# Two attention layers of a gated block: the last tiles' softmax divided after the product with the values

## The chip, the cores and the metric

The kernel runs on one core of one Trainium2 chip. The metric is the device time of one execution in microseconds. Times inside the execution are from its profile, counted from the start of the span.

## The reference

Eight sublayers work one after the other on a residual stream `x` of 4 x 256 tokens by 256 features. Each normalises the stream, computes something, and adds it back times `tanh` of a gate. The change is in the third and fourth attention (called layers 2 and 3 below); what follows them is a quantised linear layer (layer 2) and a mixture of 8 experts with a shared expert (layer 3).

```python
def _L2_xattn_ref(q, latent_kv, Wq, Wkv_expand, Wout):      # layer 3 is the same
    qp = q @ Wq.T
    k, v = jnp.split(latent_kv @ Wkv_expand.T, 2, axis=-1)
    # 16 heads of 16 features
    scores = jnp.einsum('bhqd,bhkd->bhqk', qh, kh) * inv_sqrt_d
    scores = jnp.where(causal, scores, jnp.finfo(scores.dtype).min)
    attn = jax.nn.softmax(scores, axis=-1)
    out = jnp.einsum('bhqk,bhkd->bhqd', attn, vh)
    return out.transpose(0, 2, 1, 3).reshape(b, sq, H) @ Wout.T
...
x = x + jnp.tanh(g_xattn[2]) * _L2_xattn_ref(_layernorm(x), ctx_512, ...)
x = x + jnp.tanh(g_ffn[2]) * _L2_ffn_ref(_layernorm(x), ...)       # rounds rows to int8 steps
x = x + jnp.tanh(g_xattn[3]) * _L3_xattn_ref(_layernorm(x), ctx_512, ...)
x = x + jnp.tanh(g_ffn[3]) * _L3_ffn_ref(_layernorm(x), ...)       # router, 8 experts, shared expert
```

There are 64 keys per batch, so one query tile has 16 heads x 64 keys = 1024 scores in each of its 128 rows.

## The kernel before

The 1024 tokens are 8 tiles of 128 rows, `x[0]` to `x[7]`, in two groups of four (group 0 and group 1). The residual stream stays on chip. Matrix products are in float32 unless a row says bf16.

`attention23` does layers 2 and 3. For each tile there are these steps, named as in the code:

- `scores(t)`: products of queries and keys into a PSUM tile `wide` (line 1115; on even tiles the causal mask is added by a product, line 1105), then on DVE the row maximum of each head (line 1130) and the subtraction into `attn` (line 1132, two halves), then on ACT the exponential (line 1141).
- `weights(e)`: on DVE the sum of each head (line 496) and its reciprocal (line 497), then the division of the 128x1024 tile on POOL (line 501). For the last tile half of it is done on DVE (`shared=True`).
- `transposed_pairs` (`turn`): eight 128x128 transposes on PE (line 516), copied by ACT to `attnT` (line 517), two heads in each.
- `context(t, aT)`: eight products of values with `attnT`, each 32 columns wide, into four strips of a PSUM tile `mm` (line 1148), copied by ACT to `ctxTok` (line 1157). The values are laid out block by block for two heads, so the outcome is already transposed for the next product.
- `output(cT)`: products with the output weights (line 1165); `gated_add` adds it to `x[t]` on DVE (line 527).

`in_flight_parts` writes these steps out over the tiles, with tile `t` in its turn two rounds after its scores. In the version before, tiles 0 to 4 have turn, context and output in one round; from tile 5 on, the output of a tile follows the next tile's turn. `beside` is work of other steps, one piece per round: the queries of group 1, in layer 2 also the keys and values of layer 3 (lines 1040 and 1056), and at the end of layer 2 the layer norm of group 0 (round 8) and its rounding for the quantised layer (round 9, `rounded(0)`, lines 2048 to 2055).

The framework turns this into one queue of instructions per engine, ahead of the run. What is emitted sooner has the higher priority, and among instructions that its own estimate holds ready the one of highest priority comes next; `behind(a, b)` only forces an order. On the chip each queue runs in order. Score tiles and `attnT` share six buffers (`t4`), `mm` has four PSUM buffers and `wide` has two.

`kept_busy` issues products of the identity with a weight (line 522) whose outcome is not used; there are 7 and 2 of them in the quantised layer and 1 in layer 3 at tile 2.

After layer 2 comes `ffn2`: group 0's rounded tiles are transposed and multiplied (lines 2071 and 2080), added to `x` on POOL (line 2085); then group 1 is normalised (pow on POOL, line 439; ACT, line 452), rounded and multiplied; group 0's norm for layer 3 follows (square root on ACT, line 441, reciprocal on DVE, line 444), its transposes (line 467) and queries. After layer 3 come the norms of both groups, the router (line 1199) and, beside it, the shared expert (lines 482 and 1842), then the chosen experts.

Of the kernel before, what the change touches and what calls it, by code (L numbers as in the profile page):

```python
# [30 lines left out]
F32 = mybir.dt.float32  # L31
# [5 lines left out]
ALU = mybir.AluOpType  # L37
AX = mybir.AxisListType

P = 128  # L40
B, S, D = 4, 256, 256
T = B * S
NT = T // P
TH = 512
NG = T // TH
TPG = TH // P
L, DC = 64, 64
NH, DK, CQ, CQH, R = 16, 128, 192, 96, 64
NP = NH // 2
# [48 lines left out]
def tile_flamingo(ctx: ExitStack, tc: tile.TileContext, a: dict, out: bass.AP):  # L98
    nc = tc.nc

    const = ctx.enter_context(tc.tile_pool(name="const", bufs=1))
# [4 lines left out]
    def ps_mm():  # L106
        return psum.tile([P, 512], F32, tag="mm", name="mm", bufs=4)

    def ps_wide():
        return psum.tile([P, 2, 512], F32, tag="wide", name="wide", bufs=2)  # L110

    def t4(shape, name, dtype=F32):
        return sb.tile(shape, dtype, tag="t4", name=name, bufs=6)
# [27 lines left out]
    def behind(later, sooner):  # L141

        tc.add_manual_dep(
            later.ins,
            sooner.ins.name,
            mybir.DependencyInfo(mybir.DependencyClass.NoSync, mybir.DependencyReason.DATA),
            reason="not sooner",
        )

    def side_by_side(products):  # L150

        last = None
        for product in products:
            with tc.high_priority(AT_ONCE) if last else nullcontext():
                made = product()
            if last:
                behind(made, last)
            last = made
        return last
# [26 lines left out]
    nc.gpsimd.memset(ones, 1.0)  # L186
    eps = const.tile([P, 1], F32, tag="eps", name="eps")
    nc.gpsimd.memset(eps, EPS)
    power = const.tile([P, 1], F32, tag="power", name="power")
    nc.gpsimd.memset(power, -0.5)  # L190
    root = small([P, 1], "root", 1)
# [300 lines left out]
    def weights(e, shared=False):  # L492

        groups, n = e.shape[1], e.shape[2]
        sm = sb.tile([P, 16], F32, tag="sm", name="sm", bufs=3)[:, :groups]
        nc.vector.tensor_reduce(sm, e, AX.X, ALU.add)  # L496
        made = nc.vector.reciprocal(sm, sm)  # L497
        parts = [(nc.vector, slice(0, groups // 2)), (nc.gpsimd, slice(groups // 2, groups))]
        for engine, part in parts if shared else [(nc.gpsimd, slice(0, groups))]:
            one = e[:, part]  # L500
            engine.tensor_tensor(one, one, sm[:, part].unsqueeze(2).to_broadcast(list(one.shape)), ALU.mult)  # L501
        return made
# [5 lines left out]
    def transposed_pairs(e):  # L508

        aT = t4([P, NP, P], "attnT")  # L510
        ev = e.rearrange("p h l -> p (h l)")
        for half in range(2):
            ps = ps_mm()
            for i in range(4):
                pr = half * 4 + i
                nc.tensor.transpose(ps[:, i * P : (i + 1) * P], ev[:, pr * P : (pr + 1) * P], ident)  # L516
            nc.scalar.copy(aT[:, half * 4 : half * 4 + 4, :].rearrange("p i t -> p (i t)"), ps)  # L517
        return aT

    def kept_busy(n, ps, last):  # L520
        for _ in range(n):
            made = nc.tensor.matmul(ps, ident, loaded["L3"][:, :TH], start=True, stop=True)
            behind(made, last)
            last = made

    def gated_add(t, ps, gate):
        return nc.vector.scalar_tensor_tensor(x[t], ps, gate, x[t], ALU.mult, ALU.add)  # L527
# [15 lines left out]
    def in_flight_parts(scores, turn, context, output, gate, beside):  # L543

        made, ctx, outs = {}, {}, {}

        def add(t):
            outs[t] = output(ctx.pop(t))

        for i in range(NT + 4):  # L550
            next(beside, None)
            if i < NT:
                made[i] = scores(i)
            if i >= 3 and i - 3 in outs:
                gated_add(i - 3, outs.pop(i - 3)[:, :D], gate)
            if 1 <= i <= NT:
                sums = weights(made[i - 1], shared=i == NT)
            t = i - 2
            if 0 <= t < NT:
                aT = turn(made.pop(t))  # L560
            if t >= NT - 2:
                add(t - 1)
                made_x = gated_add(t - 1, outs.pop(t - 1)[:, :D], gate)
                if t == NT - 2:
                    behind(made_x, sums)
            if 0 <= t < NT:
                ctx[t] = context(t, aT)
            if 0 <= t < NT - 3:
                add(t)
            if t == NT:  # L570
                break
# [505 lines left out]
    def attention23(layer, gate, beside):  # L1077
        kbd, vbd = kept.pop(layer)
        w = loaded[f"L{layer}"]
        w_o = w[:, 512:1024].rearrange("p (c o) -> p c o", c=2)  # L1080
        qT = []

        def queries(g):

            xn = layernorm(g, layer == 3)
            yield
            xT = transposed(xn)
            yield
            qT.append(head_queries(layer, xT))

        if (layer, 0) in kept:
            qT.append(kept.pop((layer, 0)))
        else:
            for _ in queries(0):
                pass

        def scores(t):


            g, i = divmod(t, TPG)  # L1100
            ps = ps_wide()
            masked = t % 2 == 0
            if masked:
                for a in range(2):
                    nc.tensor.matmul(
                        ps[:, a, :].rearrange("p (h l) -> p h l", l=L),
                        ident16,
                        causal16.unsqueeze(1).to_broadcast([P, 8, L]),
                        start=True,
                        stop=False,  # L1110
                    )

            def part(half, a):
                rows = slice(a * L, (a + 1) * L)
                return nc.tensor.matmul(
                    ps[:, a, half * D : (half + 1) * D],
                    qT[g][rows, half, i * P : (i + 1) * P],
                    kbd[rows, half, t // 2].rearrange("p i l -> p (i l)"),
                    start=not masked,
                    stop=(half == 1 or not masked),  # L1120
                )

            last = side_by_side(lambda half=half, a=a: part(half, a) for half in range(2) for a in range(2))
            if layer == 3 and t == 2:
                kept_busy(1, ps_mm(), last)

            e = t4([P, NH, L], "attn")
            src = ps.rearrange("p a (h l) -> p (a h) l", l=L)
            mx = small([P, NH], "mx")
            nc.vector.tensor_reduce(mx, src, AX.X, ALU.max)  # L1130
            for a in range(2):
                nc.vector.tensor_tensor(
                    e.rearrange("p (f a i) l -> p a f i l", f=2, a=2)[:, a],
                    ps[:, a, :].rearrange("p (f i l) -> p f i l", f=2, l=L),
                    mx[:, a * 8 : (a + 1) * 8]
                    .rearrange("p (f i) -> p f i", f=2)
                    .unsqueeze(3)
                    .to_broadcast([P, 2, 4, L]),
                    ALU.subtract,
                )  # L1140
            kept["exp"] = nc.scalar.activation(e, e, AF.Exp)
            return e

        def context(t, aT):
            ps = ps_mm()
            for pr in range(NP):
                half, r = divmod(pr, 4)
                nc.tensor.matmul(
                    ps[r * 32 : (r + 1) * 32, half * P : (half + 1) * P],
                    vbd[:, t // 2, pr].rearrange("p j d -> p (j d)"),  # L1150
                    aT[:, pr, :],
                    start=True,
                    stop=True,
                    tile_position=(0, r * 32),
                )
            cT = sb.tile([P, 2 * P], F32, tag="xn", name="ctxTok", bufs=AHEAD + 2)
            made = nc.scalar.copy(cT, ps[:, : 2 * P])
            if t == NT - 3:
                behind(made, kept["exp"])
            return cT  # L1160

        def output(cT):
            ps = ps_mm()
            for half in range(2):
                nc.tensor.matmul(
                    ps[:, :D], cT[:, half * P : (half + 1) * P], w_o[:, half, :], start=(half == 0), stop=(half == 1)
                )
            return ps

        in_flight_parts(scores, transposed_pairs, context, output, gate, zip_longest(queries(1), beside))  # L1170
        if layer == 3:
            used("L3")
# [1081 lines left out]
```

## Time and profile before

| what | us |
|---|---|
| median of three runs | 822.75 |
| lowest and highest | 818.82, 823.13 |
| the profiled execution | 820.13 |
| its span | 818.3 |
| PE busy | 773.3 |
| DVE busy | 502.3 |
| ACT busy | 291.1 |
| POOL busy | 242.9 |
| last exponential of layer 2 (line 1141) starts | 571.97 |
| last `gated_add` of layer 2 starts | 583.62 |
| last exponential of layer 3 starts | 634.90 |
| last `gated_add` of layer 3 starts | 646.11 |

PE is TensorE's products, PEld its loading of weights, DVE is VectorE, ACT is ScalarE, POOL is GpSimd. The span runs from the first to the last instruction; the execution's own time is 1.8 us longer. The mean granted clock of TensorE is 0.996 of full speed. Busy shares are averages over eight sublayers with different limits.

### The profile page before, as it was taken

The page shows a single profiled execution, that of the slowest core. Times are in us where ns is not written, and L with a number is a line of the kernel's source. Part 1 is how long each engine was busy: PE and PEld are TensorE (multiplying, and loading weights), DVE is VectorE, ACT ScalarE, POOL GpSimd, SP SyncE. Part 2 cuts the span into 40 slices and gives each one's busy share as a digit, 9 for nine tenths or more (in the row PEclk, how much of TensorE's full clock was granted, in tenths as well). Part 3 has the DMA queues.
Part 4 walks back from the last instruction along what each step waited for, and adds up shares of the span by engine and source line. Part 5 has one row for each costly group of instructions (what it writes and reads, how often), then busy time and mean ns, then how long its engine had stood idle before and what let it go on. Part 6 is the DMA issues. An engine that isn't in the chain of part 4 may idle for free. (4 is left out here: it accounts for less than half of the span.)

```text
span 818.3 us, 12520 instructions
## 1 busy us (share of the span) xinstructions
PE 773.3 (94%) x4509; PEld 519.4 (63%) x4512; DVE 502.3 (61%) x1154; ACT 291.1 (36%) x506; POOL 242.9 (30%) x214
## 2 busy tenths in 40 slices
PE   6999999899999899999999989999898899999994
PEld 5544433787565677676656565855445647999993
DVE  5565455876694455543878859889879664344331
ACT  2221111443421333332543459166555421233320
POOL 1454544231113244322022110015524103444332
PEclk9999999999999999999999999999999999999998
DMA  9510114800021253333740000450000102222211
GB/s 341 202 40 0 40 58 162 280 37 25 27 65 49 62 123 69 76 79 78 278 177 1 8 1 27 162 204 1 27 0 2 52 9 85 53 48 40 29 18 16
DMA packets 32467, 62.44 MB, mean 76 GB/s; under 512 B 5552, under 2 KB 19504, under 8 KB 31696
## 3 DMA queue, kind: packets, MB, share of 16 engines
q1 hardware_dynamic: 25008, 51.91, 18.5%
q0 software_dynamic: 7104, 9.41, 6.9%
q8 instruction: 39, 0.64, 0.3%
q10 hardware_dynamic: 288, 0.26, 0.1%
q14 instruction: 28, 0.23, 0.1%
HBM read 52.81 MB, written 9.27 MB: 76 GB/s over the span
## 5 line engine op out<-in xcount | busy, mean ns | idle before, releaser
L501 POOL TENSOR_TENSOR attn<-attn,sm 128x1024 f32<-128x1024 f32 (+1 forms) x32 | 55.9, 1750 | 220.4 <-DVE sm L497 176.2
L482 PE MATMUL wide<-xT,big 128*128 128x512 f32 (+1 forms) x240 | 108.6, 600 | 1.1 <-DVE shared L1724 0.9
L782 DVE TENSOR_TENSOR rope<-wide,big 128x512 f32<-128x512 f32 x96 | 59.6, 684 | 52.0 <-PE wide L482 52.0
L482 PEld LDWEIGHTS wide<-xT,big 128*128 128x128 f32 (+1 forms) x240 | 43.4, 188 | 57.3 <-issue 49.3
L1497 PE MATMUL wide<-blk,still 128*128 128x128 f32 x640 | 74.8, 275 | 0.6 <-DVE blk L1469 0.6
L1497 PEld LDWEIGHTS wide<-blk,still 128*128 128x128 f32 x640 | 73.1, 192 | 0.8 <-issue 0.8
L754 PE MATMUL mm<-vo,attnT 128*128 128x256 f32 x256 | 58.6, 382 | 1.6 <-ACT attnT L517 1.2
L482 PE MATMUL wide<-xT,dense 128*128 128x512 f32 (+1 forms) x120 | 55.2, 599 | 0.1
L754 PEld LDWEIGHTS mm<-vo,attnT 128*128 128x128 f32 x256 | 47.8, 190 | 11.5 <-issue 3.0
L517 ACT COPY attnT<-mm 128x512 f32<-128x512 f32 x64 | 34.5, 587 | 37.5 <-PE mm L516 37.1
L496 DVE TENSOR_REDUCE sm<-attn 128x16 f32<-128x1024 f32 x32 | 38.6, 1208 | 12.9 <-ACT attn L490 11.6
L1459 DVE COPY still<-big 128x1024 f32 x20 | 13.9, 693 | 52.0 <-PE wide L1497 44.5
L1531 POOL DMA_INDIRECT out_dram<-ring,scratch x20 | 31.5, 1577 | 39.5 <-DVE ring L1524 15.8
L1531 POOL DMA_INDIRECT sums<-ring,big x17 | 26.8, 1578 | 48.3 <-ACT ring L1613 18.9
L516 PE MATMUL mm<-ident,attn 128*128 128x128 f32 x256 | 34.5, 276 | 5.7 <-POOL attn L501 2.8
L1515 PE MATMUL mm<-big,hidden 128*128 x160 | 37.8, 380 | 1.4 <-DVE hidden L1508 1.4
L1432 POOL DMA_INDIRECT xs<-xd,scratch x20 | 20.0, 1000 | 62.2 <-PE mm L1466 34.1
L516 PEld LDWEIGHTS mm<-ident,attn 128*128 128x128 f32 x256 | 28.7, 141 | 14.6 <-issue 6.1
L1507 ACT ACTIVATE hidden<-wide 128x512 f32<-128x512 f32 x20 | 12.0, 598 | 71.2 <-PE wide L1497 65.7
L482 PEld LDWEIGHTS wide<-xT,dense 128*128 128x128 f32 (+1 forms) x120 | 21.5, 185 | 24.7 <-issue 22.3
L527 DVE SCALAR_TENSOR_TENSOR x<-mm,tg,x 128x256 f32<-128x256 f32 x44 | 20.6, 473 | 21.4 <-PE mm L754 12.7
L836 ACT COPY big<-mm 128x512 f32<-128x512 f32 x16 | 8.6, 589 | 68.0 <-PE mm L824 61.7
(367 smaller groups left out, 1581.8 us busy)
## 6 DMA issues: line engine op xcount, KB each, us to landing
big<-in_L_w_gate_up SPq DMA_DIRECT2D x8, 1024.0 KB, 10.4
big<-in_L_w_down SPq DMA_DIRECT2D x8, 512.0 KB, 10.7
w_L_qk<-in_L_qk SPq DMA_DIRECT2D x4, 896.0 KB, 9.6
big<-in_L_w SPq DMA_DIRECT2D x2, 1480.0 KB, 8.1
big<-in_L_w SPq DMA_DIRECT2D x2, 1110.0 KB, 5.4
big<-in_L_wo SPq DMA_DIRECT2D x1, 2048.0 KB, 15.0
big<-in_L_w SPq DMA_DIRECT2D x2, 1024.0 KB, 5.1
xd<-xn SPq DMA_DIRECT2D x16, 128.0 KB, 1.8
```

What stands on the lines that cost most here:

```text
L482: nc.tensor.matmul(ps, w(c), xT[:, c, :], start=(c == 0), stop=(c == 1))
L496: nc.vector.tensor_reduce(sm, e, AX.X, ALU.add)
L501: engine.tensor_tensor(one, one, sm[:, part].unsqueeze(2).to_broadcast(list(one.shape)), ALU.mult)
L516: nc.tensor.transpose(ps[:, i * P : (i + 1) * P], ev[:, pr * P : (pr + 1) * P], ident)
L517: nc.scalar.copy(aT[:, half * 4 : half * 4 + 4, :].rearrange("p i t -> p (i t)"), ps)
L527: return nc.vector.scalar_tensor_tensor(x[t], ps, gate, x[t], ALU.mult, ALU.add)
L754: nc.tensor.matmul(ps[:, :D], aT[:, s, :], vo[:, s, :], start=(s == 0), stop=(s == NP - 1))
L782: nc.vector.tensor_tensor(m[:, s, :].rearrange("q (b t) -> q b t", t=S), ps[:, s, :].rearrange("q (b t) -> q b t", t=S), table, ALU.mult,)
L1432: nc.gpsimd.indirect_dma_start(out=xs, out_offset=None, in_=self.xd, in_offset=bass.IndirectOffsetOnAxis(ap=self.gather[:, b : b + 1].bitc ...
L1497: made = nc.tensor.matmul(ps[:, k, f : f + P], w[:, at : at + P], st[:, c * P : (c + 1) * P], start=(c == 0), stop=(c == 1),)
L1515: made = nc.tensor.matmul(ps[:, :D], hT[:, j * P : (j + 1) * P], self.w[:, bass.ds(r + j * D, D)], start=(j == 0), stop=(j == n - 1),)
L1531: nc.gpsimd.indirect_dma_start(out=self.sums[b % len(self.sums)], out_offset=bass.IndirectOffsetOnAxis(ap=self.scatter[:, b : b + 1].bitca ...
```

## The change

The division by the softmax's sums moves for tiles 6 and 7 of both layers. `weights` is no longer called for them: their transposes take the bare exponentials. In `context` eight more products, with a 128x32 tile `pair_ones` that has ones in two blocks, put each head's sum beside its product with the values, in the other half of the same PSUM tile and in the same layout. DVE takes the reciprocal of the 128x256 sums and multiplies the 128x256 product by it; the copy on ACT is gone for these tiles.

The order of emission also moves. From tile 4 on, a tile's transposes are emitted ahead of the output of the tile before it (so far from tile 6 on). Tile 7's transposes are emitted right after tile 6's. The forced order of one `gated_add` behind the last sums goes. In layer 2 one product that is not used stands ahead of tile 6's context.

```diff
+    pair_ones = const.tile([P, 32], F32, tag="pair_ones", name="pair_ones")
+    nc.gpsimd.memset(pair_ones, 0.0)
+    nc.gpsimd.memset(pair_ones[:64, :16], 1.0)
+    nc.gpsimd.memset(pair_ones[64:, 16:], 1.0)
...
-            if 1 <= i <= NT:
-                sums = weights(made[i - 1], shared=i == NT)
+            if 1 <= i <= NT - 2:
+                weights(made[i - 1])
             t = i - 2
-            if 0 <= t < NT:
+            if 0 <= t < NT - 1:
                 aT = turn(made.pop(t))
-            if t >= NT - 2:
+            if t == NT - 2:
+                last = turn(made.pop(NT - 1))
+            if t == NT - 1:
+                aT = last
+            if t >= TPG:
                 add(t - 1)
-                made_x = gated_add(t - 1, outs.pop(t - 1)[:, :D], gate)
-                if t == NT - 2:
-                    behind(made_x, sums)
+                gated_add(t - 1, outs.pop(t - 1)[:, :D], gate)
             if 0 <= t < NT:
                 ctx[t] = context(t, aT)
-            if 0 <= t < NT - 3:
+            if 0 <= t < TPG - 1:
                 add(t)
...
         def context(t, aT):
+            if layer == 2 and t == NT - 2:
+                kept_busy(1, ps_wide()[:, 0], kept["out"])
             ps = ps_mm()
...
+            if t >= NT - 2:
+                for pr in range(NP):
+                    half, r = divmod(pr, 4)
+                    nc.tensor.matmul(
+                        ps[r * 32 : (r + 1) * 32, 2 * P + half * P : 2 * P + (half + 1) * P],
+                        pair_ones,
+                        aT[:, pr, :],
+                        start=True,
+                        stop=True,
+                        tile_position=(0, r * 32),
+                    )
+                nc.vector.reciprocal(cT, ps[:, 2 * P :])
+                nc.vector.tensor_tensor(cT, ps[:, : 2 * P], cT, ALU.mult)
+                return cT
             made = nc.scalar.copy(cT, ps[:, : 2 * P])
```

More of the change, by code (lines that the diff above doesn't have):

```diff
@@ L516, in transposed_pairs @@
                 nc.tensor.transpose(ps[:, i * P : (i + 1) * P], ev[:, pr * P : (pr + 1) * P], ident)
-            nc.scalar.copy(aT[:, half * 4 : half * 4 + 4, :].rearrange("p i t -> p (i t)"), ps)
+            kept["turned"] = nc.scalar.copy(aT[:, half * 4 : half * 4 + 4, :].rearrange("p i t -> p (i t)"), ps)
         return aT
@@ L1164, in output @@
             for half in range(2):
-                nc.tensor.matmul(
+                kept["out"] = nc.tensor.matmul(
                     ps[:, :D], cT[:, half * P : (half + 1) * P], w_o[:, half, :], start=(half == 0), stop=(half == 1)
```

## The prediction, made before the change was run

> **What bounds the kernel now.** I read the page first, then the table by windows over the two attention layers that the change touches, then the timeline of the last tiles of each, then the groups by line and shape for prices. All durations come from the profiled execution: 820.13 us, of which 818.3 is the span. The median of the three runs shown is 822.75, which is 2.62 more; a saving worked out on the trace is taken off the median.
>
> From the page (engine, busy time, share of the span, instructions):
>
> ```profile
> span 818.3 us, 12520 instructions
> PE 773.3 (94%) x4509; PEld 519.4 (63%) x4512; DVE 502.3 (61%) x1154; ACT 291.1 (36%) x506; POOL 242.9 (30%) x214
> ```
>
> PE looks like the bound everywhere, but the page's share is an average. By windows (stretch, its length, then busy time and instructions of PE, PEld, DVE, ACT and POOL, the clock, DMA):
>
> ```profile
> 575.00:580.00 5.00, 3.74 (x42) 2.38 (x41) 4.96 (x14) 3.52 (x8) 3.84 (x5) 1.00 0.00 0
> 600.00:605.00 5.00, 4.82 (x22) 2.28 (x21) 2.03 (x7) 3.48 (x8) 0.00 (x0) 1.00 0.00 0
> 630.00:635.00 5.00, 3.47 (x44) 2.09 (x36) 5.00 (x12) 2.96 (x7) 2.16 (x2) 1.00 0.02 3
> 650.00:655.00 5.00, 5.00 (x37) 4.22 (x37) 1.14 (x3) 1.93 (x3) 0.00 (x0) 1.00 0.25 81
> ```
>
> In both tails (575 and 630) DVE is full and PE waits; between the layers (600) DVE has 3 us free, waiting for queries; after layer 3 (650) PE is full. So layer 2's tail is a chain and layer 3's tail feeds a PE that has no hole afterwards: idle taken out of PE before 646 counts there in full.
>
> The tail of layer 2 (start, duration, engine, line; in brackets the idle time before it and what ended it):
>
> ```profile
> 571.97 1.06 ACT L1141 ACTIVATE attn<-attn 128x1024 f32<-128x1024 f32 x1
> ...
> 574.73 0.25 DVE L497 RECIPROCAL sm<-sm 128x16 f32<-128x16 f32 x1
> ...
> 575.17 1.54 DVE L501 TENSOR_TENSOR attn<-attn,sm 128x512 f32<-128x512 f32 x1
> ...
> 575.91 2.08 ACT L452 ACTIVATE xn<-x,shift,rstd 128x256 f32<-128x256 f32 x4
> ...
> 578.50 0.42 PE L1148 MATMUL mm<-attnT,values 128*32 128x128 f32 x8 [1.26 <-ACT attnT L517]
> ...
> 582.45 1.13 PE L1165 MATMUL mm<-w_L,ctxTok 128*128 128x256 f32 x4 [0.55 <-ACT ctxTok L1157]
> ...
> 583.62 0.48 DVE L527 SCALAR_TENSOR_TENSOR x<-mm,tg,x 128x256 f32<-128x256 f32 x1 [0.95 <-PE mm L1165]
> ...
> 593.66 0.16 DVE L444 RECIPROCAL rstd<-rstd 128x4 f32<-128x4 f32 x1
> ```
>
> The last exponential ends at 573.03, its sums and division end at 576.71, and its output starts at 582.45, because PE and ACT still work through tiles 5 and 6 and ACT normalises group 0 (575.91) ahead of tile 6's copies. x[7] is ready at 584.10. The last row is the norm that opens layer 3, in DVE's queue behind the rounding of group 1, which hangs on x[7].
>
> The tail of layer 3:
>
> ```profile
> 634.90 1.06 ACT L1141 ACTIVATE attn<-attn 128x1024 f32<-128x1024 f32 x1
> ...
> 637.04 3.35 POOL L501 TENSOR_TENSOR attn<-attn,sm 128x1024 f32<-128x1024 f32 x2 [2.83 <-DVE sm L497]
> ...
> 639.00 1.09 PE L516 MATMUL mm<-ident,attn 128*128 128x128 f32 x8 [0.72 <-POOL attn L501]
> ...
> 644.94 1.13 PE L1165 MATMUL mm<-w_L,ctxTok 128*128 128x256 f32 x4 [0.49 <-ACT ctxTok L1157]
> ...
> 646.11 0.48 DVE L527 SCALAR_TENSOR_TENSOR x<-mm,tg,x 128x256 f32<-128x256 f32 x1
> ```
>
> Here PE does wait for POOL's division (0.72), and has waits of 0.49, 0.47, 0.49, 0.29 and 0.19 for ACT's copies between 631 and 643: 2.65 in all, and 0.49 before the last output.
>
> **The change part by part.**
>
> *Taken off DVE and POOL.* Per layer two sums (1.21 each), two small reciprocals (0.25 each) and DVE's half of tile 7's division (1.54 in layer 2, 0.77 in layer 3): 4.5 and 3.7 us of DVE; POOL loses 2.95 and 3.35.
>
> *Added on DVE: the division.* Per tile one reciprocal of 128x256 out of PSUM and one product, in place of a 0.37 copy on ACT. From the groups by line and shape (count, busy, mean ns):
>
> ```profile
> L444 DVE RECIPROCAL rstd<-rstd 128x4 f32<-128x4 f32 x14 | 2.5, 175 | 7.2 <-ACT rstd L441 7.2
> L497 DVE RECIPROCAL sm<-sm 128x16 f32<-128x16 f32 x32 | 7.9, 247 | 0.4
> L1974 DVE TENSOR_TENSOR y<-mm,b 128x256 f32<-128x256 f32 x8 | 3.3, 414 | 2.0 <-PE mm L1966 2.0
> ```
>
> No reciprocal this wide is in the trace. From 4 to 16 columns it grows by 72 ns, 6.0 ns a column, so 256 columns are 175 + 252 x 6.0 = 1.69 us (estimate). The lower end is that it runs like the other 128x256 operations, 0.41; the upper takes the steepest step (128x8 at 203 ns against 128x4 at 175: 7.0 a column), 1.94. I take 1.69, since it is measured on the same operation; a product is 0.41 (L1974, also out of PSUM). A division is 2.10, between 0.83 and 2.35. Two per layer are 4.2, about what DVE loses: DVE's load is unchanged, but the work moves to the end of the chain.
>
> [...]
>
> *Added on PE.* Eight ones-products per tile cost what the context's eight cost (L1148, 0.57 from its start at 615.37 to that of the next products at 615.94): 1.14 per layer. The filler in layer 2 is a 128x512 product of 0.86 (L522: 7 in 6.17 us). It lies where PE waited 1.26 for tile 6's copies; if that wait is gone it stands ahead of context 6 with its full 0.86, and I count it so.
>
> *Moved: transposes ahead of outputs from tile 4, and 6 and 7 together.* No DMA moves. Layer 2, from the end of context 3 at 567.08, by start-to-start times: four transposes 4.12 (1.03 each), three outputs 2.91 (0.97), the values' product for layer 3 0.62, contexts 4 and 5 1.14, filler 0.86, context 6 with its ones 1.21. Sum 10.86, so context 6 ends at 577.9 if PE never waits (it ended at 579.65). Then the two divisions run one behind the other on DVE, 4.2, and the last output starts at 582.2 against 582.45: 0.3 saved. What the transposes win, the divisions spend. Queued on DVE behind the first division is the rounding of group 0 (4.5 us, 576.73 to 581.60 now) and on PE behind output 6 the last output. I take it that the rounding comes before: its norm needs POOL (pow, 1.05) and ACT, and both are freer. That is a second gain: group 0 then leaves layer 2 sooner, its norm for layer 3 passes ahead of group 1's rounding (now 2.4 us of wait, 591.23 to 593.66), and the free 3 us at 600 shrink. Between 0 and 3.0; I take 1.0, the nearest end being none, as the order of the queue is fixed ahead.
>
> *Layer 3.* PE loses 2.65 + 0.49 of waiting and gains 1.14 of work. New waits: tile 5's division on POOL ends at 634.20, while turn 4, output 3 and context 4 end at 633.25 (630.68 + 2.57), so up to 0.95; and while DVE divides tiles 6 and 7 (4.2 us) PE has context 7 and output 6, so up to 2.0 more unless the transposes and the shared expert of group 0 (645.69 to 649.2 now) move in. From -2.0 to +0.95; I take -0.8, with three fifths of the new 2.95 filled (-2.0 + 1.2).
>
> *The rest.* Three small fills on POOL at the start (rows of 0.1 to 0.2) lie beside the loads of x: nothing, 0.4 if not hidden. The context's PSUM buffer, one of four, is held 2 us longer; the next users are the transposes of what follows: in the range.
>
> Sum: -0.3 - 1.0 - 0.8 = -2.1. On the profiled execution 818.0, on the median **820.6**.
>
> **Rivals.**
>
> *Larger gain, 816.2.* The reciprocal is nearer to 0.41, or the bubble at 600 closes whole. With the bubble's whole 3.0 and layer 3's 2.0 the sum is -0.3 - 3.0 - 2.0 = -5.3; divisions of 0.83 take another 2.5 (2 x 1.27) off layer 2's chain, -7.8; the middle is -6.5. For it: DVE is free at 600. Against it: the small reciprocals' slope.
>
> *Slower, 828.4.* The rounding of group 0 gets between the two divisions. It is emitted ahead of context 7, so DVE's queue may hold division 6, rounding, division 7. With the upper price: 577.9 + 2.35 + 4.5 + 2.35 = 587.1, an output 4.7 later, and layer 3's +0.95: +5.65. It decides when group 0's norm still leaves ACT at 577.99 as now, after context 6 is done; for it, DVE is full there (4.96 of 5).
>
> *Nothing left, 823.4.* Layer 2 gains its 0.3 alone, layer 3 fills none of its waits: -0.3 + 0.95.
>
> **How the numbers follow.** A difference of 0.5% (4.1 us) is about what a measurement of this kernel can tell from none. Forecast 0.43, larger gain 0.22, nothing left 0.10, slower 0.25. The forecast's own range is 817.5 to 823.0, and 0.08 of its 0.43 lies below 818.6. Faster: 0.22 + 0.08 = 0.30; same: 0.35 + 0.10 = 0.45; slower 0.25. The range of 8 in 10 reaches to both other cases: 814.5 to 828.5.
>
> **What would show it.** Right: wide reciprocals of about 1.7 us; tile 7's transposes right behind its exponential; context 6 of layer 2 done near 578; x[7] within half a microsecond of 584.1 and 646.6; the clock at 1.00. Wrong: wide reciprocals under 1 or over 2 us; rounding rows (L2053) between the two divisions; DVE's free time at 600 gone or grown; PE idle of 2 us before layer 3's last output.

## The result and the profile after

The changed kernel takes 830.48 us (median of 4 runs, 827.93 to 833.92), the kernel before 821.57 beside it: a ratio of 1.0118, 95% interval 1.0084 to 1.0152. It is slower, by 8.9 us. The forecast was 820.6, with 814.5 to 828.5 as its range: wrong in sign and outside the range.

The profiled execution after took 827.93 us. From its page (engine, busy time, share of the span, instructions):

```profile
span 826.1 us, 12633 instructions
PE 777.8 (94%) x4578; PEld 523.8 (63%) x4578; DVE 504.6 (61%) x1152; ACT 289.7 (35%) x502; POOL 237.2 (29%) x213
```

The shares are within a point of those before, so the page alone does not say where 7.8 us of span went. A table of stretches does. It is measured from four events that both traces have: the first product of scores of a layer, the start of its last `gated_add`, and the router's first maximum (line 492 here, 488 before).

| stretch, us | before | after | difference |
|---|---|---|---|
| start to first scores of layer 2 | 537.49 | 536.53 | -0.96 |
| first scores to last `gated_add`, layer 2 | 46.13 | 49.61 | +3.48 |
| from there to first scores of layer 3 | 19.08 | 19.09 | +0.01 |
| first scores to last `gated_add`, layer 3 | 43.41 | 48.27 | +4.86 |
| from there to the router | 8.31 | 8.73 | +0.42 |
| router to the end | 163.88 | 163.87 | -0.01 |

The first row lies ahead of everything that was changed; it varies between 535.7 and 540.0 over the kernels below. The loss is in the two tails, and none of it comes back. Two of the windows that the prediction showed, in the changed kernel (stretch, length, busy time and instructions of PE, PEld, DVE, ACT, POOL, the clock, DMA):

```profile
575.00:580.00 5.00, 2.70 (x38) 1.57 (x36) 4.90 (x14) 1.10 (x3) 0.58 (x1) 1.00 0.00 0
650.00:655.00 5.00, 3.48 (x13) 2.81 (x13) 3.23 (x9) 0.59 (x1) 0.00 (x0) 0.55 0.31 105
```

In layer 2's tail DVE is as full as before (4.90 against 4.96), but PE does 1.04 us less. Behind layer 3, where PE had been full, it now idles 1.52 us of 5, and its clock is 0.55.

The timeline of layer 2's tail (start, duration, engine, line; idle time before it and what ended it):

```profile
574.70 1.13 PE L1187 MATMUL mm<-w_L,ctxTok 128*128 128x256 f32 x4 [1.05 <-ACT attnT L521]
...
577.23 0.48 DVE L2077 TENSOR_SCALAR xn<-xn 128x256 bf16<-128x256 f32 x2
...
578.18 1.73 DVE L1176 RECIPROCAL ctxTok<-mm 128x256 f32<-128x256 f32 x1
579.94 0.42 DVE L1177 TENSOR_TENSOR ctxTok<-mm,ctxTok 128x256 f32<-128x256 f32 x1
580.51 1.10 PE L1187 MATMUL mm<-w_L,ctxTok 128*128 128x256 f32 x4 [2.81 <-DVE ctxTok L1177]
581.55 0.64 PE L1156 MATMUL mm<-attnT,values 128*32 128x128 f32 x16
582.01 0.62 PE L1168 MATMUL mm<-attnT,pair_ones 128*32 128x128 f32 x16
582.74 1.73 DVE L1176 RECIPROCAL ctxTok<-mm 128x256 f32<-128x256 f32 x1
...
584.97 1.13 PE L1187 MATMUL mm<-w_L,ctxTok 128*128 128x256 f32 x4 [2.35 <-DVE ctxTok L1177]
585.94 0.81 PE L2093 MATMUL mm<-ident,xn 128*128 128x128 bf16 x8
586.14 0.48 DVE L531 SCALAR_TENSOR_TENSOR x<-mm,tg,x 128x256 f32<-128x256 f32 x1 [1.22 <-PE mm L1187]
```

Read it downwards as one chain. The first row is output 5, which waited 1.05 for ACT's copies to `attnT`; the second is the end of group 0's rounding. From reciprocal 6 on, PE waits 2.81 for division 6, does output 6, and only then context 7 and its ones (581.55, 582.01); they free DVE for division 7, and PE waits again, 2.35. The two divisions do not run one behind the other: output 6 stands between them in PE's queue. The rounded tiles of group 0 have been ready since 577.7 (line 2077), but their transposes (line 2093) stand behind output 7.

The same in layer 3:

```profile
643.93 1.76 DVE L1176 RECIPROCAL ctxTok<-mm 128x256 f32<-128x256 f32 x1 [0.35 <-PE mm L1168]
...
646.21 1.13 PE L1187 MATMUL mm<-w_L,ctxTok 128*128 128x256 f32 x4 [2.34 <-DVE ctxTok L1177]
...
650.63 0.32 DVE L459 TENSOR_SCALAR xn<-x,mv,rstd 128x256 f32<-128x256 f32 x1
...
651.42 2.04 PE L1187 MATMUL mm<-w_L,ctxTok 128*128 128x256 f32 x4 [2.52 <-DVE ctxTok L1177]
...
653.50 0.48 DVE L531 SCALAR_TENSOR_TENSOR x<-mm,tg,x 128x256 f32<-128x256 f32 x1 [1.26 <-PE mm L1187]
```

Group 0's normalised tiles (line 459), which could have fed PE, are queued behind reciprocal 7. And the last output takes 2.04 where that of layer 2 took 1.13: the clock was at 0.50. Two windows of 3.41 us, ahead of a fall of the clock and behind it:

```profile
582.79:586.20 3.41, 1.23 (x9) 1.03 (x10) 2.15 (x4) 0.00 (x0) 0.00 (x0) 1.00 0.00 0
586.20:589.61 3.41, 3.16 (x17) 1.90 (x15) 2.17 (x8) 1.84 (x4) 1.28 (x2) 0.50 0.49 154
```

The price of the division itself, from the groups (count, busy, mean ns):

```profile
L1176 DVE RECIPROCAL ctxTok<-mm 128x256 f32<-128x256 f32 x4 | 7.0, 1742 | 0.8 <-PE mm L1168 0.8
```

The product with it takes 423 ns. Both are as predicted (1.69 and 0.41).

### The profile page after: what moved, and what is told of

It reads as the page before. It is cut to its first block, busy times and chain, and to the rows that moved or that the text cites. A ratio compares the mean times of both kernels' runs of the same rounds, so it can differ in the third digit from the quotient of the medians.

```text
span 826.1 us, 12633 instructions
## 1 busy us (share of the span) xinstructions
PE 777.8 (94%) x4578; PEld 523.8 (63%) x4578; DVE 504.6 (61%) x1152; ACT 289.7 (35%) x502; POOL 237.2 (29%) x213
## 5 line engine op out<-in xcount | busy, mean ns | idle before, releaser
L505 POOL TENSOR_TENSOR attn<-attn,sm 128x1024 f32<-128x1024 f32 (+1 forms) x28 | 49.7, 1775 | 214.9 <-DVE sm L501 181.3
L760 PEld LDWEIGHTS mm<-vo,attnT 128*128 128x128 f32 x256 | 47.8, 190 | 11.5 <-issue 3.0
L500 DVE TENSOR_REDUCE sm<-attn 128x16 f32<-128x1024 f32 x28 | 33.8, 1208 | 11.9 <-ACT attn L494 11.6
```

Of the source, the lines that this page charges most:

```text
L760: nc.tensor.matmul(ps[:, :D], aT[:, s, :], vo[:, s, :], start=(s == 0), stop=(s == NP - 1))
```

## The experiments

Three causes could make up the loss, and each can be taken away alone. *Order*: output 6 stands between the contexts on PE, so the divisions cannot overlap with PE's work. *Clock*: PE's clock is at 0.50 behind its waits, which stretches its rows (2.04 for an output instead of 1.13). *Price*: 1.74 us of reciprocal on a chain where ACT's copy took 0.37. A fourth question is what the new order of emission does without the division. The stretches of all kernels, in us, their medians, and their ratios to the kernel before on the same chip (its medians there 820.3 to 821.6):

| kernel | tail of layer 2 | to layer 3 | tail of layer 3 | to router | median | ratio (95%) |
|---|---|---|---|---|---|---|
| before | 46.13 | 19.08 | 43.41 | 8.31 | 821.57 | |
| after | 49.61 | 19.09 | 48.27 | 8.73 | 830.48 | 1.0118 (1.0084 to 1.0152) |
| e1, context 7 first | 48.93 | 19.06 | 46.18 | 9.15 | 825.69 | 1.0057 (1.0035 to 1.0079) |
| e2, order alone | 47.11 | 19.06 | 44.65 | 8.31 | 822.84 | 1.0029 (1.0008 to 1.0049) |
| e3, division alone | 51.47 | 20.50 | 47.39 | 8.33 | 831.11 | 1.0131 (1.0095 to 1.0167) |
| e4, waits filled | 49.62 | 19.08 | 46.80 | 8.21 | 827.10 | 1.0068 (1.0045 to 1.0091) |
| e5, copy for reciprocal | 46.94 | 20.59 | 44.23 | 8.40 | | |
| e6, divisions in order | 48.29 | 19.07 | 45.45 | 9.78 | 826.00 | 1.0049 (1.0012 to 1.0086) |
| e7, tile 6 alone | 49.19 | 19.08 | 44.94 | 8.32 | 824.66 | 1.0053 (1.0036 to 1.0071) |
| e8, outputs later | 44.22 | 21.72 | 42.58 | 8.28 | 821.32 | 1.0003 (0.9985 to 1.0021) |
| e9, e6 filled | 47.35 | 19.07 | 44.50 | 9.33 | 822.98 | 1.0043 (1.0024 to 1.0063) |
| e10, e8 and norm first | 44.22 | 21.41 | 42.85 | 8.28 | 819.59 | 0.9996 (0.9979 to 1.0014) |
| e11, e9 and ones first | 47.35 | 20.66 | 44.50 | 9.33 | 823.43 | 1.0032 (1.0010 to 1.0054) |
| e12, e10 filled | 44.20 | 21.99 | 42.58 | 8.28 | 820.62 | 0.9991 (0.9976 to 1.0006) |

The stretches come from one profiled execution of each kernel, the ratios from 4 to 12 runs of it. The longer ways to layer 3 in e3, e5 and e11 (20.50 to 20.66 against 19.1) go with a half clock between the layers: 599.94 to 603.36, 596.26 to 599.67 and 598.78 to 602.20 in their traces.

**e1: context 7 ahead of output 6.**

```diff
+            if t == NT - 1:
+                ctx[t] = context(t, aT)
             if t >= TPG:
                 add(t - 1)
                 gated_add(t - 1, outs.pop(t - 1)[:, :D], gate)
-            if 0 <= t < NT:
+            if 0 <= t < NT - 1:
                 ctx[t] = context(t, aT)
```

> The changed kernel with one move: tile 7's context is emitted ahead of tile 6's output, in both layers, so TensorE's queue holds context 6, context 7, output 6, output 7. Theory ORDER (the loss is that output 6 stands between the two contexts, so that division 7 can only start after division 6, output 6 and context 7; from the end of ones-product 6 to the start of output 7 it took 7.27 us in layer 2 and 7.55 in layer 3, where two divisions of 2.15 back to back would take 4.4): 2.8 us less per layer, waits of TensorE near 1 us each, so the clock holds too; 5.5 to 7 us less than the changed kernel, within 0.3% of the kernel before. Theory PRICE (a reciprocal of 1.74 is too dear at the end of the chain in any order): at most 2 us less, still 0.8% over before. Theory CLOCK (the time goes by TensorE's clock at 0.5 in 586 to 589 and 647 to 654 us): follows the clock; if it still falls, the time stays.

The loss halves. What is left shows at once on the timeline:

```profile
578.52 3.34 DVE L1178 RECIPROCAL ctxTok<-mm 128x256 f32<-128x256 f32 x2
...
582.28 3.50 PE L1189 MATMUL mm<-w_L,ctxTok 128*128 128x256 f32 x8 [3.38 <-DVE ctxTok L1179]
```

With both contexts done, DVE's queue holds both reciprocals ("x2", 3.34) ahead of the first product. Output 6 now waits 3.38 instead of 2.81: the stall moved from PE's queue into DVE's, and the clock fell here too (0.50 from 582.55 to 585.96).

**e6: e1, and reciprocal 7 behind product 6.**

```diff
-                nc.vector.reciprocal(cT, ps[:, 2 * P :])
-                nc.vector.tensor_tensor(cT, ps[:, : 2 * P], cT, ALU.mult)
+                turned_over = nc.vector.reciprocal(cT, ps[:, 2 * P :])
+                if t == NT - 1:
+                    behind(turned_over, kept["divided"])
+                kept["divided"] = nc.vector.tensor_tensor(cT, ps[:, : 2 * P], cT, ALU.mult)
```

> Context 7 ahead of output 6, as in the run before, and on VectorE the product of tile 6 forced ahead of the reciprocal of tile 7 (there the two reciprocals ran first, so that output 6 waited 3.4 and 3.0 us). Theory ORDER in its second form (two queues hold the tail back, TensorE's and VectorE's): from ones-product 6 to the last gated_add 5.6 us, TensorE's waits near 1.2 us, the clock at 1.00; 2 to 4 us less than with context 7 first alone, within 0.3% of before. Theory PRICE: two divisions of 2.2 still follow each other after the last context, so the tail stays 1.2 to 1.6 us longer per layer than before: 0.3 to 0.5% over before.

Both tails shorten again, by 0.64 and 0.73, and the waits are now what is left when PE's work is used up:

```profile
583.36 1.10 PE L1191 MATMUL mm<-w_L,ctxTok 128*128 128x256 f32 x4 [1.94 <-DVE ctxTok L1181]
585.57 2.08 PE L1191 MATMUL mm<-w_L,ctxTok 128*128 128x256 f32 x4 [1.10 <-DVE ctxTok L1181]
```

The second output takes 2.08, in a clock of 0.50 from 584.69 to 591.52: it fell behind shorter waits too. The median did not follow the tails (826.0, with runs from 820.5 to 828.8), so e6 against e1 is not told apart by their times.

**e4: the changed kernel, two unused products behind the ones of each tile.** `summed` is the last product with ones.

```diff
+                kept_busy(2, ps_wide()[:, 0], summed)
                 nc.vector.reciprocal(cT, ps[:, 2 * P :])
```

> The changed kernel with two unused 128x512 products (0.88 us each) behind each ones-product, in TensorE's waits for the four divisions (2.35 to 2.81 us each); everything else and the order stay. Theory CLOCK: the clock stays at 1.00 in both tails and most of the loss goes, 5 us or more less than the changed kernel. Theory ORDER: the clock stays at 1.00, but the chain from ones-product 6 to output 7 keeps its 7.3 us; only what the half clock stretched comes back, 1 to 3 us.

The clock stays at 1.00. In the window around layer 3's tail, first the changed kernel, then e4:

```profile
640.00:660.00 20.00, 14.63 (x130) 10.96 (x127) 11.72 (x25) 5.64 (x11) 0.00 (x0) 0.83 0.16 53
```

```profile
640.00:660.00 20.00, 18.30 (x161) 12.13 (x160) 12.84 (x33) 7.16 (x13) 0.00 (x0) 1.00 0.15 51
```

Layer 3 gains 1.47 in its tail and 0.52 on the way to the router, layer 2 nothing: there the clock fell at 586.2, when the last `gated_add` had already begun. So the clock is worth 2.0 us in the profile; the medians differ by 3.4, and no stretch shows the rest. Output 6 still starts 2.80 us behind tile 6's ones in layer 2 (2.81 in the changed kernel), because what fills a wait does not shorten it.

**e9: e6 with its waits filled.** Order and clock together.

```diff
                 add(t - 1)
+                if t == NT - 1:
+                    kept_busy(1, ps_wide()[:, 0], kept["out"])
                 gated_add(t - 1, outs.pop(t - 1)[:, :D], gate)
...
                 if t == NT - 1:
                     behind(turned_over, kept["divided"])
+                    kept_busy(2, ps_wide()[:, 0], summed)
```

> The kernel of e6 with unused 128x512 products in its waits: two behind the ones-products of tile 7, one behind output 6. Theory of three causes (order of the queues, clock, length of the division): the clock stays at 1.00 in both ends; first scores to last add 47.8 to 48.3 us in layer 2 (e6: 48.29, before: 46.13) and 44.0 to 44.7 in layer 3 (e6: 45.45, before: 43.41), add to router 8.3 to 8.6 (e6: 9.78); median about 823.5, 0.3 to 0.4% above before: what is left is the division itself. Rival (order and clock explain all of the loss, the division costs nothing once they are mended): 46.1 and 43.4, median 821. Rival (the clock is only a sign, not a cause): the three stretches stay as in e6, median 826.

The clock is 1.00 through both tails, and the divisions now run as the prediction had assumed:

```profile
579.78 1.72 DVE L1180 RECIPROCAL ctxTok<-mm 128x256 f32<-128x256 f32 x1
581.54 0.42 DVE L1184 TENSOR_TENSOR ctxTok<-mm,ctxTok 128x256 f32<-128x256 f32 x1
581.88 1.75 DVE L1180 RECIPROCAL ctxTok<-mm 128x256 f32<-128x256 f32 x1
...
584.32 1.13 PE L1194 MATMUL mm<-w_L,ctxTok 128*128 128x256 f32 x4 [0.25 <-DVE ctxTok L1184]
```

Tails of 47.35 and 44.50. e4 and e9 both keep the clock and differ in the order: it is worth 2.27 in layer 2 and 2.30 in layer 3. Layer 2 beats what was expected (47.8 to 48.3), since the clock had cost something there as well: the last output takes 1.13 here, 2.08 in e6. What remains against the kernel before is 1.22 and 1.09, and the ratio, 1.0043, is still above 1: with order and clock both mended, the change gains nothing.

**e5: a copy in place of the reciprocal.**

```diff
-                nc.vector.reciprocal(cT, ps[:, 2 * P :])
+                nc.vector.tensor_copy(cT, ps[:, 2 * P :])
```

> The changed kernel with a copy of the 128x256 sums in place of their reciprocal, so the last two tiles are multiplied by their sums and not divided; all else and the order stay. The copy should be 0.42 us, like other 128x256 copies out of PSUM, against 1.74. Theory PRICE (the length of the reciprocal at the end of the chain): from the end of ones-product 6 to the last gated_add 5.8 us instead of 8.44 in layer 2, TensorE's waits near 1.1 us, the clock at 1.00 in both tails; 6 to 9 us less than the changed kernel, within 0.3% of before. Theory ORDER (output 6 between the contexts): 2.6 us less in each tail by the shorter divisions, but the serial order stays, 4 us less in all.

With other values in the stream what follows the router takes 190.4 instead of 163.9 us (median 849.16), presumably because its experts get other loads, so only the stretches ahead of it are compared. A copy takes 0.40 where the reciprocal took 1.74. The tails are 46.94 and 44.23, shorter by 2.67 (2.68 for two times 1.34) and by 4.04 (the clock's part included), and still above those before. So in this order the reciprocal's length is spent in full, twice per layer; yet a division as cheap as a copy would not have made this order a gain.

**e11: e9 with the ones-products ahead of the values'.** The loop over `pair_ones` moves above the loop over `values`.

> The kernel of e9 with the ones-products of tiles 6 and 7 ahead of their values' products. Theory: reciprocal 6 starts 0.46 to 0.64 sooner, and the chain reciprocal, product, reciprocal, product (4.2) moves with it: first scores to last add 0.4 to 0.6 under e9 in each layer, median about 822.7. Rival (TensorE's queue, not VectorE's chain, sets the last output): no difference to e9.

The rival was right: 47.35 and 44.50, to the last digit those of e9. In layer 3 the reciprocal still starts only when the values' products have ended:

```profile
645.58 0.64 PE L1161 MATMUL mm<-attnT,pair_ones 128*32 128x128 f32 x16 [0.41 <-ACT attnT L521]
646.04 0.62 PE L1171 MATMUL mm<-attnT,values 128*32 128x128 f32 x16
...
646.73 1.76 DVE L1181 RECIPROCAL ctxTok<-mm 128x256 f32<-128x256 f32 x1 [0.35 <-PE mm L1171]
```

It reads only the ones' half of the PSUM tile, and is released by the values' half (line 1171). In layer 2 DVE itself is not free sooner: it rounds group 0 until the reciprocal starts. The reason that the expectation gave, PE's queue, is not what the rows show.

**e2 and e3: each half of the change alone.** e2 keeps the new order and divides ahead of the transposes, as before, so `context` has neither the block under `if t >= NT - 2` nor the unused product of layer 2; e3 keeps the old order and divides tiles 6 and 7 behind, without that unused product.

```diff
# e2, against the changed kernel
-            if 1 <= i <= NT - 2:
-                weights(made[i - 1])
+            if 1 <= i <= NT:
+                weights(made[i - 1], shared=i == NT)
# e3, against the changed kernel
-            if 0 <= t < NT - 1:
+            if 0 <= t < NT:
                 aT = turn(made.pop(t))
-            if t == NT - 2:
-                last = turn(made.pop(NT - 1))
-            if t == NT - 1:
-                aT = last
-            if t >= TPG:
+            if t >= NT - 2:
                 add(t - 1)
...
-            if 0 <= t < TPG - 1:
+            if 0 <= t < NT - 3:
                 add(t)
```

> The order of emission alone: transposes ahead of outputs from tile 4 on and 6 and 7 together, but all tiles are divided before their transposes as in the kernel before (tile 7 half on VectorE, half on GpSimd), no ones-products, no filler, and the forced order of the gated_add is gone. Theories ORDER, PRICE and CLOCK, which all put the loss on the division behind the product: no loss, 0 to 3 us less than before. Theory MOVE (transposes ahead of outputs are what costs, since the copies and the softmax of the next tiles come in another order): 4 us or more over before.

> The division behind the product alone: tiles 6 and 7 of both layers as in the changed kernel, but the order of emission of the kernel before (tile 7's transposes in its own round) and no filler; the forced order of the gated_add is gone with the sums. TensorE's queue holds ones 6, transposes 7, output 6, context 7, ones 7, output 7, so one wait is filled with 1.0 us of transposes. Theory ORDER: the second division still starts behind output 6; 5 to 9 us over before. Theory PRICE: 4 reciprocals, of which about half is exposed, 4 to 5 us over before. Theory MOVE: 2 us over before at most. Theory CLOCK: 8 or more only if the clock falls below 0.9 again in the two tails.

The division alone is as bad as the whole change (1.0131), so the new order is not what makes it slow. That is 10.8 us over before, more than theories ORDER, PRICE and MOVE had (9 at most); and theory CLOCK's condition was not met, since the clock stayed at 1.00 through both tails, which grew by 5.34 and 3.98. The order alone is slightly slower too (1.0029, 2.5 us), where three theories had no loss and the fourth 4 us. Tile 7's transposes, emitted with tile 6's, wait for their own division while output 5 is ready behind them:

```profile
576.34 0.64 PE L520 MATMUL mm<-ident,attn 128*128 128x128 f32 x4 [1.70 <-DVE attn L505]
```

**e7: the old order, tile 6 alone divided behind**, tile 7 as before: the least that can be changed.

```diff
-            if 1 <= i <= NT:
+            if 1 <= i <= NT and i != NT - 1:
                 sums = weights(made[i - 1], shared=i == NT)
...
+            if t == NT - 2:
                 for pr in range(NP):
```

> The order of emission of the kernel before; tile 6 alone is divided behind the product, tile 7 before its transposes, shared by VectorE and GpSimd as in the kernel before. The division of tile 6 lies beside the transposes of tile 7 (1.0 us) and output 6 waits for the rest, about 1 us; tile 7's division no longer stands behind tile 6's on GpSimd (1.90). Theory PRICE: only a division that has nothing beside it costs, so this is within 0.3% of before, 1 us less at best in each layer. Theory ORDER: the same, if no output stands between a context and its division. Theory CLOCK: any wait of TensorE above 2 us here lets the clock fall and costs 1 to 2 us.

Output 6 in layer 2:

```profile
584.46 1.10 PE L1183 MATMUL mm<-w_L,ctxTok 128*128 128x256 f32 x4 [2.08 <-DVE ctxTok L1173]
```

The ratio is 1.0053, with the clock at 1.00; the expectation, within 0.3% of before, did not come true. The division of tile 6 starts in layer 2 0.5 us after its sums are there, since the rounding of group 0 is ahead of it on DVE, and output 6 then waits 2.08 there, with the clock at 1.00 behind it, against theory CLOCK, and 1.32 in layer 3. One division is enough to cost 4 us.

**e8, e10 and e12: the part of the order that gains.** e8 is the kernel before with outputs moved behind the next tile's transposes from tile 4 on, and no pairing of tiles 6 and 7.

```diff
# e8, against the kernel before
-            if t >= NT - 2:
+            if t >= TPG:
...
-            if 0 <= t < NT - 3:
+            if 0 <= t < TPG - 1:
                 add(t)
# e10, against e8
-        unit(0, turned(xq), xs)
-        xq, xs = rounded(1)
+        xqT = turned(xq)
+        xn = layernorm(1, True, powered=True)
+        unit(0, xqT, xs)
+        xq, xs = rounded(1, xn)
# e12, against e10
-            kept_busy((7, 2)[g], ps_wide()[:, 0], last)
+            kept_busy((9, 2)[g], ps_wide()[:, 0], last)
```

> The kernel before with one part of the change's order: from tile 4 on the transposes are emitted ahead of the output of the tile before; tile 7's transposes stay in their own round, the division and the forced order stay as before. In the run of the order alone tile 7's transposes waited 1.70 and 1.51 us for their division ahead of outputs that were ready. Theory MOVE: if the pairing of tiles 6 and 7 was what cost 0.3% there, this is 1 to 3 us less than before, since the waits of 0.49 for the copies go; if the outputs' place itself costs, it is 1 to 2 us over before.

Both tails shorten, by 1.92 and 0.83, and nothing arrives at the end (1.0003): the way from layer 2 to layer 3 grows by 2.64. (The expectations of e10 and e12 count from the `gated_add` of `x[6]`, which runs 0.4 us ahead of the last one here: their 2.31, 22.11 and 21.81 are 1.92, 21.72 and 21.41 in the table.) POOL behind layer 2's tail, first in the kernel before, then in e8:

```profile
585.07 1.02 POOL L439 TENSOR_TENSOR rstd<-rstd,power 128x4 f32<-128x4 f32 x1 [5.70 <-DVE rstd L438]
...
586.83 2.78 POOL L2085 TENSOR_TENSOR x<-x,y 128x256 f32<-128x256 f32 x4 [0.74 <-DVE y L2084]
```

```profile
584.07 2.77 POOL L2085 TENSOR_TENSOR x<-x,y 128x256 f32<-128x256 f32 x4 [3.89 <-DVE y L2084]
586.80 1.03 POOL L439 TENSOR_TENSOR rstd<-rstd,power 128x4 f32<-128x4 f32 x1
```

In the kernel before, the power for group 1's norm (line 439) ran at 585.07, ahead of group 0's adds (line 2085, 586.83); in e8 these stand ahead of it. Group 1 is normalised later, PE waits 2.32 for its rounding, and its clock halves from 594.20 to 597.61.

> The kernel of e8 (outputs later from tile 4 on, tile 7's transposes in their own round, nothing else) with the normalisation of tiles 4 to 7 handed in ahead of the products of group 0 in the unit of 8-bit weights. Theory: e8 lost its 2.31 us of layer 2 because VectorE had group 0's four scaled adds (1.66) ahead of the variance of tiles 4 to 7, and GpSimd group 0's four adds (2.77) ahead of their power, so that TensorE waited 2.32 and then ran 594 to 598 at 0.55 to 0.60 of its clock; with the order mended the last add of layer 2 to the first scores of layer 3 takes 19.1 to 19.8 (e8: 22.11, before: 19.08), first scores to last add stay at 43.8 and 42.6, and the median is 818 to 819, 0.3 to 0.4% under before. Rival (the way from layer 2 to layer 3 is bound by group 0's products and adds, which begin no sooner): 21 to 22, median as e8, 821.3.

> The kernel of e10 with nine instead of seven unused 128x512 products behind group 0's products in the unit of 8-bit weights (0.88 us each, so 1.76 of the 1.93 us that TensorE waits there). Theory: what e8 and e10 lose between the layers is now mostly the clock (0.50 to 0.72 in 592 to 596 of e10: its second group's products, fillers and the way to the first scores took 5.94 us from 591.76 to 597.70, where before took 4.04 from 594.70 to 598.74); with the clock kept the last add of layer 2 to the first scores of layer 3 falls from 21.81 to 19.9 to 20.2, and the median is about 818, 0.2 to 0.3% under before. Rival (the clock falls all the same, or the added products stand in the way): 21.5 to 22.5, median 820, no difference to before.

e10 puts the power first (581.55), and gains 0.31 of the 2.64: the wait is 1.93, and the clock still falls, to 0.92 in 590 to 592 and 0.50 in 592 to 594. e12 fills that wait to 0.22, and the clock falls all the same, 594.73 to 598.14, in a later wait of 1.23. In both the way to layer 3 is where the rival had put it (21.41 and 21.99), and the ratios, 0.9996 and 0.9991, have intervals that hold 1. No kernel here beats the one before by more than the measurement can tell.

## Why the prediction was wrong

- **The price of a division** (1.69 + 0.41 estimated from the slope of two small reciprocals): right, 1.742 + 0.423.
- **Context 6 of layer 2 ends at 577.9**: 577.70, but the stretch began 0.96 sooner, so by the clock of the trace before it is 578.66, 0.76 late. The sum held only "if PE never waits", and PE waited 1.05 ahead of output 5 (574.70) for ACT's copies to `attnT`, which ran behind ACT's normalisation of group 0 (line 456, 572.10 to 574.19). The other terms together were some 0.4 shorter than summed.
- **"Then the two divisions run one behind the other on DVE, 4.2, and the last output starts at 582.2": the step that failed.** It counted the divisions on DVE and forgot PE's queue, in which output 6 and context 7 follow each other as they are emitted. From the end of tile 6's ones to the start of output 7 were 7.27 us in layer 2 (577.70 to 584.97) and 7.55 in layer 3 (643.87 to 651.42): division, output and context, division. The prediction even named "context 7 and output 6" as PE's work during the divisions, in the wrong order: output 6 cannot lie beside division 6. e1 and e6 put context 7 first, and e9 against e4 shows the worth of the order: 2.3 us per layer.
- **The clock at 1.00**, given as a sign of being right, was not priced as a risk. It cost 2.0 us (e4). Its falls, at 586.20 and 647.63, come 1.2 and 1.4 us behind the waits of 2.35 (layer 2) and 2.34 (layer 3) that the failed step hid.
- **"Group 0 leaves layer 2 sooner", -1.0**: the condition came true and the gain did not. Group 0 was rounded at 577.7 instead of 581.60, but its transposes stand behind output 7 on PE, and the way from the last `gated_add` to layer 3 is 19.09 against 19.08. The step named the queue ("on PE behind output 6 the last output") and took the gain anyway.
- **Layer 3, -0.8, "three fifths of the new 2.95 filled"**: nothing was filled. What should have filled it was queued on DVE behind reciprocal 7 (line 459 at 650.63). The tail grew by 4.86. POOL's wait for tile 5 (up to 0.95) was 0.91, as priced.
- **The slower rival, 828.4**, was near the measured time for another reason. Its mechanism, rounding between the two divisions, did not happen: the rounding was done before reciprocal 6 began.

Sizes: of the 8.34 us that the tails grew, order is 4.57 (e9 against e4) and the clock 1.46 (e4 against the change, layer 3's tail; another 0.52 lies behind it).

The 2.31 that e9 leaves can be read from the lines of e9 and the kernel before, counted from the layer's first scores. Context 6, in e9 with its ones, ends 1.00 sooner in layer 2 and 0.19 in layer 3 (41.16 against 42.16, 38.63 against 38.82): that is what the transposes win. From there to the start of the last output it takes 5.02 instead of 2.80, and 4.73 instead of 3.42, with two divisions on the chain: 2.22 and 1.31 more. So in e9's order the divisions still spend more than the earlier transposes win. Against the prediction's own sum for layer 2 (last output 44.71 after the first scores) e9 is 1.47 late: context 6 by 0.75, 0.48 until DVE, behind rows of rounding and norms, begins reciprocal 6, and 0.24 in the divisions themselves.

How much of the 2.31 is the price of the reciprocal itself is not shown: in favour of the division's length speaks e5, in the change's order; but e2, with no division behind, lies 0.98 and 1.24 above the tails before, so the pairing of tiles 6 and 7 could make up as much of it. e2 also lost clock, from 576.8 to 580.2, so the two stay unseparated.

e9 and e11 also take 1.0 longer to the router and 1.6 less behind it. In part that is work of the shared expert (line 486 in e9, 482 before) done sooner: ahead of group 1's transposes e9 has six of its rows (2.84 us from 650.24), the kernel before four (1.98 from 647.29). The rest stays open.

## What to carry to other kernels

When work moves from a free engine onto the chain of the last tiles, write down both queues instruction by instruction, and ask of each wait what stands next behind it on the same engine: here the divisions overlapped with nothing while the consumer of the first was queued ahead of the producer of the second (7.27 us from tile 6's ones to the last output of layer 2, 5.02 in e9's order). A gain at one place is only worth what the next queue lets through, so follow it until it reaches the end or a wait (e8: 2.75 us gained in two tails, 2.64 lost in between). Price a halved clock where an edit adds waits to TensorE: here the clock fell behind stretches of 3.41 us of which PE was busy 0.98 to 1.70, though not behind all such, and cost the changed kernel 2.0 us.

## What the runs showed of the hardware

**The half clock lasted 3.41 or 6.83 us here.** By half-microsecond windows, the stretches at 0.50 last 3.41 (after layer 2: 586.20 to 589.61), 6.83 (after layer 3: 647.63 to 654.46), 3.41 (e1: 582.55 to 585.96), 6.83 (e6: 584.69 to 591.52), 3.41 (e8) and 3.41 (e12), and 3.41 for the second of e1 and e6 and for those of e2, e3, e5, e10 and e11: once or twice 3.41 wherever the clock fell between 500 and 700 us.

Ahead of the falls, PE was busy 1.23, 1.43, 1.25, 0.98 and 1.70 of the 3.41 us just before (changed kernel twice, e6, e8, e12); the window from 575.97 to 579.38 of the changed kernel, with 1.73, was followed by full speed. None of these falls had a wait of 3.41 ahead of it: the longest single waits in these five windows were 1.23 to 2.35, while the wait of 2.81 in layer 2, which lies across two such stretches (busy 1.73 and 2.11), was followed by full speed.

The busy share alone does not tell the falls: e3 kept its clock behind a window with 1.55 (586.29 to 589.70), and e3 and e5 lost it behind windows that PE's rows fill (661.38 to 664.79 and 654.29 to 657.70, with transposes and the router's products of 128x8 among them).

The length of the waits does not tell them either. At the rounding of group 1 the kernel before waits 0.96, 0.50 and 0.57 and keeps its clock, e12 waits 0.22, 0.50 and 1.23 and loses it. And e9 and e11 have the same rows on PE, within 0.01 us, from the last `gated_add` of layer 2 until e11's clock falls, with waits of 0.96, 0.50 and 0.57 in both. e11 falls at 598.78, behind 3.41 us with 1.38 busy, and its next products take 1.74 and 2.99; e9 keeps its clock behind the same rows, and they take 1.21 and 1.88. The way to layer 3 is 20.66 in e11 and 19.07 in e9: the same waits cost 1.59 or nothing.

In three kernels the falls of one execution lie whole multiples of 3.41 apart: in the changed kernel, at 586.20, 647.63 and 818.30, by 61.43 and 170.67 (18.0 and 50.0 times), in e1, at 582.55 and 647.40, by 64.85, and in e6, at 584.69 and 649.56, by 64.87 (19.0 times each). Whether that has to do with what a wait costs, no run here shows.

**A reader of half a PSUM tile waited for the other half.** In layer 3 of e11 tile 6's reciprocal of 256 columns (646.73) started only after the products into the other 256 columns of the same tile had ended, 0.07 us after them. Whether the chip asks for that, or only the waits that the framework put into the queues, no run here shows.
